# Moving the side pieces of an LSTM stage to other places, starting two chunks a round earlier, and building the length-1 weight sums in the layer that uses them

## The chip, the cores and the metric

One core of one Trainium2 chip runs the whole kernel as one program. The metric is the device time of that program in microseconds (us); lower is better. All matrices are float32.

The engines are named as the profile names them: PE (matmuls; PEld is its weight load), DVE (VectorE), ACT (ScalarE), POOL (GpSimd) and SP (SyncE, which only issues transfers here). Each takes its own instructions in the order of the program. A "manual schedule" in the kernel means that this order is the order in which the Python code emits the instructions.

## The reference, cut to what matters

Four residual layers act on x of shape 128 x 64 x 256 (8192 tokens of width 256). The change touches the second layer and its border with the first:

```python
# layer 1 (the second): h is relu(layernorm(x)), adj is 64 x 64
h = relu(einsum('ts,bsh->bth', adj, h @ Wg0 + bg0))
h = relu(einsum('ts,bsh->bth', adj, h @ Wg1 + bg1))
for p in range(1, 5):                       # four LSTMs, one after the other
    nw = T // p
    wins = h[:, :nw * p, :].reshape(B * nw, p, H)      # windows of p tokens
    last = lstm_last(Wih[p-1], Whh[p-1], bih[p-1], bhh[p-1], wins)
    h[:, arange(nw) * p + p - 1, :] = last             # overwrites the last token of a window
x = x + h
```

Layer 0 is a graph convolution with two batch norms, layer 2 causal attention, layer 3 masked attention with four heads. Each LSTM rewrites part of h before the next one reads it, so for one piece of data the four are a chain.

## The kernel before

The 8192 tokens are 16 chunks of 512. In layer 1 two chunks form a superchunk; there are eight, sc = 0 to 7. The LSTM code of a superchunk is the main stream. It is a Python generator that yields at 22 **places**, 0 to 21. At a place the main loop puts pieces of a second stream between the LSTM instructions: the two graph convolutions of the next superchunk's chunks, the residual sum of the last superchunk's, and the normalization that layer 2 will need. Length 1 has places 0 to 3, length 2 has 4 to 7, length 3 has 8 to 13, length 4 has 14 to 21.

```python
def convolutions(c):                      # 14 pieces, c0 to c13
    y, h = conv_tile(c)                   # c0: tag "cv", 2 buffers
    for m in range(KD): scaled(y, c, m)   #     two DVE operations
    mid = res.tile(...)                   #     two DVE transposes into mid
    far = put(mid, f"y{c}"); get(dst, far)      # store to DRAM, load back in token order
    nc.sync.dma_start(xs[c], xr[c])             # load x
    yield
    add_squares(xs[c], xs[c], dst); yield       # c1: DVE, needs both loads
    stats = ln_stats(xs[c], f"b{c}"); yield     # c2: DVE, then POOL (1/sqrt)
    yield from apply_halves(h, xs[c], stats, f"b{c}")   # c3, c4: ACT; c3 begins with nmr on DVE
    banks = aggregate(h, adjt_bd, f"b{c}"); yield       # c5: PE, 64 small matmuls
    ...copy on DVE...; yield                            # c6
    banks = product_v(c, y); yield                      # c7: PE, 3.4 us
    bounded(y, banks); yield                            # c8: DVE
    banks = product_u(c, y); yield                      # c9: PE, 3.4 us
    biased(h, banks); yield                             # c10: DVE
    banks = aggregate(h, adjt_bd, f"c{c}"); yield       # c11: PE
    for e, ps in enumerate(banks): to_hT(c, e, ps); yield   # c12, c13: ACT

def ahead(c):                             # 6 pieces, h0 to h5, for layer 2
    # h0 put, h1 load back, h2 statistics (DVE, POOL), h3 and h4 apply (ACT),
    # h5 four DVE transposes and a put

def residual(c, hT):                      # r0 transposes (DVE) and put, r1 load, r2 add
```

An LSTM step of length p works on "units", one for each gate and step. Each unit forms its product by a seven-product block scheme whose partial results lie in a few PSUM banks (tags x, y, z with two banks each), so that PE can go on only after ACT or DVE has read a bank:

```python
for s in range(1, p):
    last = s == p - 1
    B = [Unit(q, s) for q in (1, 3)]
    ...
    each(A, pe(5, "h"), do("copy", 5), pe(1), do("copy", 1), pe(3, "h"), pe(6, "x"), pe(6, "h"),
         pe(2, "h"), do("u4"), do("c11"), do("c12"))     # copy: ACT (L1155); u4, c11..: DVE (L1158)
    each(B, pe(5), do("copy", 5))
    each(A, do("act", 0), pe(7), do("c22"), do("act", 1))      # act: ACT (L1063)
    ...
    each(B, pe(1), do("copy", 1))
    yield                                                # a place in the middle of a step
    ...cells, tanh, new_state on DVE and ACT...
            new_state(s, 1, halves[1])
            ...
            new_state(s, 1, halves[0])
            if last: load_sets(2)
            else:    dh[2]()
    yield                                                # a place at the end of a step

def new_state(s, c, part):     # last step: the new h, written into the sequence
    ...
    nc.vector.tensor_mul(tokens(c, s, j), folded(gate(3, c, part)), folded(gate(2, c, part)))
```

The tables of places, and their use for superchunk sc:

```python
RESIDUAL = (0, 3, 4), (2, 5, 6)                 # chunks of sc - 1
CONV = (4, 4, 5, 6, 7, 8, 9, 10, 10), (6, 8, 9, 9, 10, 11, 12, 13, 14, 15, 16, 17, 18, 20)
                                                # first (A) and second (B) chunk of sc + 1
BEGUN = 13, 15, 16, 17, 18                      # first chunk of sc + 2
AHEAD = (4, 5, 10, 12, 14, 18), (6, 7)          # chunks of sc - 1
LATE = 4, 5, 6, 7                               # rest of the second chunk of sc - 2
```

The length-1 LSTM has no recurrent term. Its weights and their four block sums are `wih1`. They are made in layer 0, with those of the other lengths, and stored to DRAM; layer 1 loads them. At the border of the layers the product of two attention weights is also stored, and the first convolution reuses its memory:

```python
wanted = [(p, (wih_t, q), (whh_t, q)) for p in range(2, SKIP + 1) for q in GATES]
wanted[6:6] = [(1, (wih_t, GATES[0]), (wih_t, GATES[1]))]
wanted[7:7] = [(1, (wih_t, GATES[2]))]
...
nc.sync.dma_start(products_far, wqkv_sb[:, :, : 2 * D])     # in weight_products()
...
wih1 = w1.tile([P, 3, 7, P], F32, name="wih1")
for i, q in enumerate(GATES[:3]):
    nc.sync.dma_start(wih1[:, i], wfar[1, q])
```

Of the kernel before, what the change touches and what calls it, by code (L numbers as in the profile page):

```python
# [8 lines left out]
F32 = mybir.dt.float32  # L9
# [10 lines left out]
def kernel(  # L20
# [666 lines left out]
    with tc.manual_schedule(engines={mybir.EngineType.PE}):  # L687
# [30 lines left out]
        def weight_products():  # L718
            for m in range(KD):
                ps = bank(f"c1_{m}")  # L720
                nc.tensor.matmul(ps[:, :P], bg0_sb[:, m * P : (m + 1) * P], adjt_bd, start=True,
                                 stop=True)
                nc.scalar.copy(c1[:, m, :], ps[:, :P])
                nc.scalar.mul(nc1[:, m, :], ps[:, :P], -1.0)
            for a in range(KD):
                for dst, lhs, rhs in ((products[0], 0, wt[:, KD : 2 * KD, :]),
                                      (products[1], 2 * KD, wo_sb)):
                    ps = bank(f"wp_{a}_{lhs}")
                    for f in range(KD):
                        nc.tensor.matmul(ps[:, :D], wt[:, lhs + f, a * P : (a + 1) * P],  # L730
                                         rhs[:, f, :], start=(f == 0), stop=(f == KD - 1))
                    nc.scalar.copy(dst[:, a, :], ps[:, :D])
            nc.sync.dma_start(products_far, wqkv_sb[:, :, : 2 * D])
            ps = bank("c2")
            for k in range(KD):
                nc.tensor.matmul(ps[:, :D], c1[:, k, :], wg1_st[:, k, :], start=(k == 0),
                                 stop=(k == KD - 1))
            return ps

        def weight_sums(p, *sources):
            n = len(sources)
            name = "_".join(f"{p}{q}" for _, q in sources)
            w = stage.tile([P, 16, P], F32, tag="ws", name=f"ws_{name}", bufs=2)
            for i, (src, q) in enumerate(sources):
                nc.sync.dma_start(
                    w[:, 8 * i : 8 * i + 4, :].rearrange("p (k c) f -> p k (c f)", k=KD),
                    src[p - 1].rearrange("(k p) f -> p k f", p=P)[:, :, q * D : (q + 1) * D])
            yield  # L750
            v = w.rearrange("p (i b) f -> p i b f", i=2)[:, :n]
            for dst, a, b, op in ((4, 1, 3, OP.add), (5, 4, 0, OP.subtract), (6, 0, 1, OP.subtract),
                                  (7, 2, 5, OP.subtract)):
                nc.gpsimd.tensor_tensor(v[:, :, dst], v[:, :, a], v[:, :, b], op)
            if p == 1:
                for i, (_, q) in enumerate(sources):
                    far = dram.tile([P, 7, P], F32, tag=f"ws{p}{q}", name=f"wfar_{p}_{q}", bufs=1)
                    nc.sync.dma_start(far[:, :1], w[:, 8 * i : 8 * i + 1])
                    nc.sync.dma_start(far[:, 1:], w[:, 8 * i + 2 : 8 * i + 8])
                    wfar[p, q] = far  # L760
            else:
                far = dram.tile([P, 15, P], F32, tag=f"ws{p}{q}", name=f"wfar_{p}_{q}", bufs=1)
                nc.sync.dma_start(far[:, :9], w[:, :9])
                nc.sync.dma_start(far[:, 9:], w[:, 10:])
                wfar[p, q] = far
            yield

        wanted = [(p, (wih_t, q), (whh_t, q)) for p in range(2, SKIP + 1) for q in GATES]
        wanted[6:6] = [(1, (wih_t, GATES[0]), (wih_t, GATES[1]))]
        wanted[7:7] = [(1, (wih_t, GATES[2]))]  # L770
    tc.no_sync_barrier()


    with tc.manual_schedule(engines={mybir.EngineType.PE, mybir.EngineType.DVE,
# [2 lines left out]
        sevens[2].relu(2, 3, 0, 1)  # L777
        for c in range(2, NCH - 1):
            a, b, z = sevens[c], sevens.get(c + 1), sevens.get(c - 1)
            weights = [weight_sums(*wanted.pop(0)) for _ in range(1 + (len(wanted) == 7)) if wanted]  # L780
            for w in weights:
                next(w)
            a.product(2, "Z")
            if c == 2:
                a.begin()
# [36 lines left out]
            else:  # L822
                new_h1(c + 1)
                for k in range(KH):
                    relu2(c + 1, k)
            for w in weights:
                next(w)
            a.product(3, "Y")
            a.add(0, 1, "Y")
            if b:  # L830
# [38 lines left out]
    nc.sync.dma_start(bias2, bhh)  # L869

    wih1 = w1.tile([P, 3, 7, P], F32, name="wih1")
    for i, q in enumerate(GATES[:3]):
        nc.sync.dma_start(wih1[:, i], wfar[1, q])

    coming = [(p, q) for _ in range(NCH // SUP) for p in range(2, SKIP + 1) for q in GATES]
    wsets = {}
# [141 lines left out]

    BLOCKS = {1: (0, 8), 2: (2, 9), 3: (7, 14), 4: (3, 10), 5: (4, 11), 6: (5, 12), 7: (6, 13)}

    def lstm(p, hv, name):


        nb = hv.shape[3]
# [16 lines left out]
        def folded(t):  # L1041
            return t.rearrange("p (a b) -> p a b", b=inner)
# [16 lines left out]
        def gate(q, c, part=slice(0, n)):  # L1059
            return gates[:, q, c, part]  # L1060
# [5 lines left out]
        halves = [slice(0, m), slice(m, n)]  # L1066
        every = slice(0, n)

        def new_state(s, c, part):

            if s < p - 1:
                nc.vector.tensor_mul(hn[:, c, part], gate(3, c, part), gate(2, c, part))
            elif part == every:
                nc.vector.tensor_mul(natural(hv[:, c, cols(s), :]), columns_of(gate(3, c)),  # L1074
                                     columns_of(gate(2, c)))
            else:
                j = halves.index(part)
                nc.vector.tensor_mul(tokens(c, s, j), folded(gate(3, c, part)),
                                     folded(gate(2, c, part)))

        def operands_x(s):

# [111 lines left out]
        for s in range(1, p):  # L1194
# [48 lines left out]
            new_state(s, 1, halves[1])  # L1243
            if not last:
                dh[1]()
            new_state(s, 1, halves[0])
            if last:
                load_sets(2)
            else:
# [124 lines left out]
    def lstms(sc, hT):  # L1374
        hv = hT.rearrange("p k (t b) -> p k t b", t=T)

        def views(part):
            return {(k, j): part(hv[:, k, j * T // 2 : (j + 1) * T // 2, :]) for k in range(KD)
                    for j in range(2)}

        if sc:
            yield from single(views(lambda a: a.rearrange("p t b -> p (t b)")), CH, f"{sc}_1", range(4))
        else:
            for i in range(SUP):
                yield from single(views(lambda a: a[:, :, i * NB : (i + 1) * NB]), CH // 2, f"{sc}_1_{i}",
                                  (1, 3))
        for p in range(2, SKIP + 1):
            yield from lstm(p, hv, f"{sc}_{p}")

    def new_hT(sc):  # L1390

# [48 lines left out]


    RESIDUAL = (0, 3, 4), (2, 5, 6)
    CONV = (4, 4, 5, 6, 7, 8, 9, 10, 10), (6, 8, 9, 9, 10, 11, 12, 13, 14, 15, 16, 17, 18, 20)
    BEGUN = 13, 15, 16, 17, 18
    FIRST = (0, 2, 3, 4, 4, 5, 6, 7, 8, 9, 10, 11, 12, 12), (3, 6, 7, 8, 8, 13, 14, 15, 16, 17, 18, 19, 20, 20)
    AHEAD = (4, 5, 10, 12, 14, 18), (6, 7)
    LATE = 4, 5, 6, 7
    IDLE = {5: 4, 7: 18, 9: 10, 13: 14, 15: 8}
    FINAL = (4, 5, 10, 12, 12, 14), (6, 7, 11, 14, 14, 16)
    START = (0, 1, 0, 0, 0, 1, 0, 1, 1, 0, 0, 1, 1, 0, 1)  # L1450
# [2 lines left out]
    with tc.manual_schedule(engines={mybir.EngineType.PE, mybir.EngineType.DVE, mybir.EngineType.Pool,  # L1453
# [5 lines left out]
        for n, i in enumerate(START):  # L1459
# [5 lines left out]
                    keep_busy(fill, name)  # L1465
            next(convs[i])
            if n == 1:
                load_sets(6)
    banks_of("psum1", x=2, y=2, z=2, ps=2)
    tc.no_sync_barrier()  # L1470
    with tc.manual_schedule(engines={mybir.EngineType.PE, mybir.EngineType.DVE, mybir.EngineType.Pool,
                                     mybir.EngineType.Activation, mybir.EngineType.SP}):
        last = NCH // SUP - 1
        for sc in range(last + 1):
# [21 lines left out]
                for i in range(SUP):  # L1496
                    units((FINAL if sc == last else AHEAD)[i], aheads[(sc - 1) * SUP + i])
            if sc + 1 < last:
                units(BEGUN, convs[(sc + 2) * SUP])
            for n, _ in enumerate(lstms(sc, hTs[sc])):  # L1500
                for u in todo.pop(n, ()):
                    next(u)
# [537 lines left out]
```

## Time and profile before

| quantity | value |
|---|---|
| device time, median of 3 | 1962.3 us (1960.02 to 1969.14) |
| span of the profiled execution | 1964.6 us |
| PE busy | 1879.6 us, 96% of the span |
| DVE, ACT, POOL busy | 1263.7, 1015.8, 567.9 us |
| layer 1 LSTMs, sc = 0 to 7 | about 296 to 1590 us of the span |
| one middle superchunk | about 164 to 167 us |

A row of the timeline gives start, duration, engine, line, operation, what it writes and reads, and how many equal ones were merged. The bracket at its end is the time for which the engine stood idle before it, and the instruction that ended this idle time. "DMA" as the releaser means a transfer that landed. PEclk in the table of windows is the share of full TensorE clock that was granted.

### The profile page before, as it was taken

Reading aid. Unit: us, or ns where it says so; the run is one execution under the profiler, and the core shown is the slowest. Engines: PE = TensorE matmul, PEld = TensorE weight load, DVE = VectorE, ACT = ScalarE, POOL = GpSimd, SP = SyncE. Lnnn points to the kernel's source line nnn. Section 1 sums busy time; section 2 is a strip of 40 time slices with the busy share of each in tenths; the row PEclk is TensorE's granted clock in tenths of the full one; section 3 lists DMA queues with packets and bytes.
Section 4 is the critical chain, followed back from the end, with each engine's and each line's share of the span. In section 5 each row is a group of like instructions: output and inputs, shape, how many; then the busy total and the mean of one; then the engine's idle time right before and its main releaser. Section 6 shows DMA issues by size and latency. Waiting matters only on the chain.

```text
span 1964.6 us, 39217 instructions
## 1 busy us (share of the span) xinstructions
PE 1879.6 (96%) x15119; PEld 1494.1 (76%) x15119; DVE 1263.7 (64%) x3164; ACT 1015.8 (52%) x2309; POOL 567.9 (29%) x763
## 2 busy tenths in 40 slices
PE   8999979999999999999999999999999999999998
PEld 6877756886787788588678768858968976777776
DVE  6768635556556756666665666666565657667776
ACT  5766426456355445544645555554464544444453
POOL 5756512222212121222212212122132213223332
PEclk9999989999999999999999999999999999999999
DMA  3224552134432432443353233244235335444433
GB/s 111 75 65 177 196 212 71 75 113 141 139 113 103 118 125 81 145 145 113 124 177 113 92 115 134 85 145 145 81 124 166 100 93 164 143 141 130 151 115 113
DMA packets 112219, 244.23 MB, mean 124 GB/s; under 512 B 11552, under 2 KB 74912, under 8 KB 112032
## 3 DMA queue, kind: packets, MB, share of 16 engines
q1 hardware_dynamic: 111280, 240.37, 36.3%
q8 instruction: 120, 1.97, 0.4%
q0 software_dynamic: 320, 1.05, 0.2%
q14 instruction: 67, 0.55, 0.1%
q10 hardware_dynamic: 432, 0.30, 0.1%
HBM read 171.88 MB, written 69.80 MB: 123 GB/s over the span
## 4 chain that ended last, share of the span: by engine, by line
PE 69%; DVE 9%; ACT 5%; DMA 2%; issue 2%; POOL 1%; SPq 0%; DVEq 0%; ACTq 0%; POOLq 0%
PE x L1149 19%; PE z L1149 9%; PE g L1120 8%; PE v L1530 5%; PE y L1149 5%; PE x L1304 3%; PE p_q L1537 3%; PE u L924 3%; PE v L910 3%; PE X L1726 2%; PE y L1304 2%; DVE cell L1217 1%; DVE cell L1216 1%; PE Y L1726 1%; DVE gates L1158 1%
## 5 line engine op out<-in xcount | busy, mean ns | idle before, releaser
L1158 DVE TENSOR_TENSOR gates<-gates,x 128x128 f32<-128x128 f32 (+2 forms) x384 | 119.3, 322 | 323.7 <-PE x L1149 316.0
L1149 PE MATMUL x<-xd,wset 128*128 128x128 f32 (+2 forms) x1280 | 288.3, 313 | 37.4 <-ACT gates L1155 27.8
L1207 POOL TENSOR_TENSOR gates<-gates 128x512 f32<-128x512 f32 (+2 forms) x48 | 76.7, 1599 | 628.8 <-ACT gates L1063 628.8
L1149 PE MATMUL x<-hd,wset 128*128 128x128 f32 (+2 forms) x1152 | 248.5, 305 | 0.0
L1149 PEld LDWEIGHTS x<-xd,wset 128*128 128x128 f32 x1280 | 203.5, 191 | 58.3 <-ACT gates L1155 21.2
L1063 ACT ACTIVATE gates<-gates,bias 128x256 f32<-128x256 f32 (+4 forms) x384 | 169.9, 490 | 61.7 <-DVE gates L1158 59.3
L1149 PEld LDWEIGHTS x<-hd,wset 128*128 128x128 f32 x1152 | 186.7, 193 | 5.0
L1120 PE MATMUL g<-hT,wset 128*128 128x256 f32 (+2 forms) x576 | 184.1, 474 | 1.2 <-DVE hT L1074 1.1
L1120 PEld LDWEIGHTS g<-hT,wset 128*128 128x128 f32 x576 | 108.5, 190 | 70.0 <-issue 39.5
L1149 PE MATMUL z<-hs,wset 128*128 128x128 f32 (+2 forms) x768 | 155.6, 305 | 0.0
L1155 ACT COPY gates<-y 128x128 f32<-128x128 f32 (+2 forms) x192 | 53.4, 293 | 189.7 <-PE y L1149 189.0
L1149 PEld LDWEIGHTS z<-hs,wset 128*128 128x128 f32 x768 | 121.4, 193 | 3.3
L1107 ACT ACTIVATE gates<-g,bias 128x512 f32<-128x512 f32 (+2 forms) x144 | 76.9, 562 | 67.8 <-PE g L1120 67.3
L1158 DVE TENSOR_TENSOR gates<-gates,z 128x128 f32<-128x128 f32 (+2 forms) x384 | 104.8, 316 | 1.0 <-PE z L1149 0.9
L1155 ACT COPY gates<-x 128x128 f32<-128x128 f32 (+2 forms) x192 | 55.5, 297 | 87.6 <-PE x L1149 87.1
L1063 ACT ACTIVATE gates<-x,bias 128x128 f32<-128x128 f32 (+2 forms) x192 | 74.8, 390 | 50.2 <-PE x L1149 47.4
L1149 PE MATMUL z<-hT,wset 128*128 128x128 f32 (+1 forms) x512 | 97.1, 302 | 0.0
L1218 ACT ACTIVATE gates<-cell 128x256 f32<-128x256 f32 (+2 forms) x144 | 55.2, 384 | 70.2 <-DVE cell L1217 70.1
L1149 PE MATMUL x<-hs,wset 128*128 128x128 f32 (+2 forms) x384 | 84.9, 303 | 0.0
L313 POOL TENSOR_TENSOR xd<-hT 128x128 f32<-128x128 f32 (+3 forms) x57 | 38.4, 674 | 160.0 <-DVE hT L1074 100.5
L1149 PE MATMUL y<-hd,wset 128*128 128x128 f32 (+2 forms) x384 | 81.2, 314 | 0.0
L1149 PE MATMUL y<-xd,wset 128*128 128x128 f32 (+2 forms) x384 | 78.6, 307 | 2.1 <-ACT gates L1107 2.1
(324 smaller groups left out, 4291.0 us busy)
## 6 DMA issues: line engine op xcount, KB each, us to landing
wset<-wfar SPq DMA_DIRECT2D x96, 960.0 KB, 6.5
hT<-far_h SPq DMA_DIRECT2D x124, 128.0 KB, 3.2
far_h<-hm SPq DMA_DIRECT2D x16, 512.0 KB, 2.8
far_n<-xs SPq DMA_DIRECT2D x16, 512.0 KB, 4.2
xs<-far_n SPq DMA_DIRECT2D x64, 128.0 KB, 3.5
far_x<-xs SPq DMA_DIRECT2D x16, 512.0 KB, 3.0
x<-far_x SPq DMA_DIRECT2D x64, 128.0 KB, 3.2
xt<-in_x_dram SPq DMA_DIRECT2D x15, 512.0 KB, 4.0
```

What stands on the lines that cost most here:

```text
L910: nc.tensor.matmul(banks[m], wg0_sb[:, k, m * P : (m + 1) * P], agg[:, k, :], start=(k == 0), stop=(k == KD - 1))
L924: nc.tensor.matmul(banks[j // 2][:, j % 2, :], v[:, k, j * P : (j + 1) * P], wg1_sb[:, k, :], start=(k == 0), stop=(k == KD - 1))
L1063: nc.scalar.activation(gate(q, c, part), src, AF.Tanh if q == 2 else AF.Sigmoid, bias=bs[:, q * KD + c : q * KD + c + 1])
L1107: nc.scalar.activation(columns_of(gate(q, c)), natural(banks[q, c][:, :n].rearrange("p (w b) -> p w b", b=nb)), AF.Tanh if q == 2 else AF. ...
L1120: nc.tensor.matmul(banks[q, c][:, :n].rearrange("p (w b) -> p w b", b=nb), wsets[p, q][:, 2 * k + c, :], hv[:, k, : (nw - 1) * p + 1 : p, ...
L1149: nc.tensor.matmul(folded(self.psum(kind)), wsets[p, self.q][:, BLOCKS[kind][i], :], (ox[self.s] if part == "x" else oh)[kind], start=firs ...
L1155: nc.scalar.copy(gate(self.q, kind // 5, halves[kind // 5]), self.psum(kind))
L1158: nc.vector.tensor_add(gate(self.q, *dst), gate(self.q, *a), self.psum(kind))
L1207: nc.gpsimd.tensor_mul(gates[:, 0, :, :n], gates[:, 0, :, :n], gates[:, 2, :, :n])
L1304: nc.tensor.matmul(folded(ps(g, kind)), wih1[:, g, KINDS1[kind], :], right[kind], start=kind in (2, 5, 1), stop=True, skip_group_check=True)
L1530: nc.tensor.matmul(ps[:, i, :], hT[:, k, j, :], w[:, k, first : first + D], start=(k == 0), stop=(k == KD - 1))
L1726: nc.tensor.matmul(st[c, tag][:, i * CH // 2 : (i + 1) * CH // 2].rearrange("p (a n) -> p a n", n=P), w, st[c, "o7"][kind], start=first an ...
```

## The change

It has four parts.

1. The tables of places are rewritten. No place holds the statistics of a chunk together with the scaling that needs them, and several pieces move by one to six places.
2. Both chunks of sc + 2, not only the first, are begun one superchunk ahead: the first with pieces c0 to c3 (before: c0 to c4), the second with c0 and c1.
3. The very last state multiplication of length 4 runs on POOL instead of DVE where another superchunk follows.
4. The length-1 weight sums leave layer 0. Layer 1 loads the raw weights while its first convolutions run, and POOL forms the four sums there. The store of the attention products is issued from ACT's queue instead of SP's.

The place tables, and what lies at each place in a middle superchunk (A, B: chunks of sc + 1; A', B': of sc + 2; R: residual; H0, H1: the two chunks of sc - 1; L: the late chunk):

| place | before | after |
|---|---|---|
| 3 | R0.r1 | A.c4, B.c2, R0.r1 |
| 4 | L.h2, A.c5, A.c6, R0.r2, H0.h0 | A.c5, A.c6, B.c3, B.c4, R0.r2, H0.h0 |
| 5 | A.c7, R1.r1, L.h3, H0.h1 | L.h2, A.c7, R1.r1, H0.h1 |
| 6 | A.c8, B.c0, R1.r2, L.h4, H1.h0 | A.c8, R1.r2, L.h3, H1.h0 |
| 7 | A.c9, L.h5, H1.h1 | A.c9, H0.h2, H1.h1 |
| 8 | A.c10, B.c1 | A.c10, L.h4, H0.h3 |
| 9 | A.c11, B.c2, B.c3 | A.c11, L.h5 |
| 10 | A.c12, A.c13, B.c4, H0.h2 | A.c12, A.c13 |
| 11 | B.c5 | B.c5, A'.c0 |
| 12 | B.c6, H0.h3 | B.c6 |
| 13 | B.c7, A'.c0 | B.c7, A'.c1 |
| 14 | B.c8, H0.h4 | B.c8, H0.h4, A'.c2 |
| 15 | B.c9, A'.c1 | B.c9, H0.h5 |
| 16 | B.c10, A'.c2 | B.c10, A'.c3 |
| 17 | B.c11, A'.c3 | B.c11, B'.c0 |
| 18 | B.c12, H0.h5, A'.c4 | B.c12 |
| 19 | | B'.c1 |
| 20 | B.c13 | B.c13 |

The diff, cut to its core:

```diff
-            nc.sync.dma_start(products_far, wqkv_sb[:, :, : 2 * D])
+            nc.scalar.dma_start(products_far, wqkv_sb[:, :, : 2 * D])
...
-        wanted[6:6] = [(1, (wih_t, GATES[0]), (wih_t, GATES[1]))]
-        wanted[7:7] = [(1, (wih_t, GATES[2]))]
...
-    for i, q in enumerate(GATES[:3]):
-        nc.sync.dma_start(wih1[:, i], wfar[1, q])
+    def load_single():
+        rest = ...                        # the memory of an LSTM cell tile
+        for g, q in enumerate(GATES[:3]):
+            raw = wih_t[0].rearrange("(k p) (q f) -> p k q f", p=P, f=D)[:, :, q]
+            nc.sync.dma_start(wih1[:, g, 0], raw[:, 0, :P])
+            nc.sync.dma_start(rest[:, g], raw[:, 0, P:])
+            nc.sync.dma_start(wih1[:, g, 1:3], raw[:, 1].rearrange("p (c f) -> p c f", c=KD))
+        yield
+        w = wih1.rearrange("p g s f -> p s g f")
+        for dst, a, b, op in ((3, rest, w[:, 2], OP.add), (4, w[:, 3], w[:, 0], OP.subtract),
+                              (5, w[:, 0], rest, OP.subtract), (6, w[:, 1], w[:, 4], OP.subtract)):
+            nc.gpsimd.tensor_tensor(w[:, dst], a, b, op)
+        yield
...
-            new_state(s, 1, halves[0])
+            new_state(s, 1, halves[0], nc.gpsimd if follows and last else nc.vector)
...
-    CONV = (4, 4, 5, 6, 7, 8, 9, 10, 10), (6, 8, 9, 9, 10, 11, 12, 13, 14, 15, 16, 17, 18, 20)
-    BEGUN = 13, 15, 16, 17, 18
+    CONV = (3, 4, 4, 5, 6, 7, 8, 9, 10, 10), (3, 4, 4, 11, 12, 13, 14, 15, 16, 17, 18, 20)
+    BEGUN = (11, 13, 14, 16), (17, 19)
+    BEGUN_FIRST = (13, 15, 16, 18), (19, 21)              # used in sc = 0
-    AHEAD = (4, 5, 10, 12, 14, 18), (6, 7)
-    LATE = 4, 5, 6, 7
+    AHEAD = (4, 5, 7, 8, 14, 15), (6, 7)
+    LATE = 5, 6, 8, 9
...
+                singles = load_single()                   # n == 1 of the first convolutions
+                next(singles)
                 load_sets(6)
+            if n == 9:
+                next(singles)
```

## The prediction

> **What bounds the kernel now.** I read the busy times by engine first. PE is busy for 1879.6 of 1964.6 us, so the whole kernel has some 85 us of PE idle time, and the other engines matter only where they make PE wait. Then I cut the span by stage, with the table of windows (columns: stretch, its length, busy time and instructions of PE, PEld, DVE, ACT, POOL, then PEclk, DMA share, GB/s):
>
> ```profile
> 223.00:260.00 37.00, 26.73 (x114) 19.66 (x112) 17.74 (x40) 12.11 (x28) 13.66 (x19) 0.91 0.62 216
> 313.00:460.00 147.00, 142.62 (x1062) 120.59 (x1063) 82.93 (x240) 73.56 (x190) 33.68 (x47) 1.00 0.26 94
> 627.00:794.00 167.00, 159.66 (x1092) 129.21 (x1091) 106.56 (x282) 86.09 (x211) 38.23 (x51) 0.98 0.36 123
> 959.00:1123.00 164.00, 156.66 (x1092) 126.30 (x1091) 106.32 (x282) 86.11 (x211) 38.05 (x51) 1.00 0.36 125
> 1448.00:1590.00 142.00, 139.33 (x817) 115.44 (x815) 84.21 (x243) 80.77 (x196) 32.46 (x45) 1.00 0.35 111
> ```
>
> A middle superchunk loses about 7.3 us of PE (164 - 156.66), the first and last 3 to 4, the border of layers 0 and 1 about 10. DVE and ACT have room on average, so a wait can only come from their order. The timeline of PE alone gives each wait by name; one superchunk (sc = 3) has these, and they repeat to 0.02 us in sc = 1 to 5:
>
> ```profile
> 795.65 1.12 PE L1304 MATMUL x<-hT,wih 128*128 128x512 f32 x2 [0.90 <-ACT gates L1063]
> 868.11 1.49 PE L1149 MATMUL x<-xd,wset 128*128 128x168 f32 x4 [3.28 <-ACT gates L1155]
> 883.36 0.55 PE L1149 MATMUL x<-xd,wset 128*128 128x168 f32 x2 [0.85 <-DVE gates L1158]
> 931.64 0.68 PE L1149 MATMUL x<-xd,wset 128*128 128x128 f32 x4 [1.63 <-ACT gates L1155]
> 942.31 0.49 PE L1149 MATMUL x<-xd,wset 128*128 128x128 f32 x2 [0.43 <-DVE gates L1158]
> ```
>
> The full timeline around each says why. For the largest:
>
> ```profile
> 864.47 0.23 POOL L99 TENSOR_SCALAR rstd_b<-mv_b 128x4 f32<-128x4 f32 x1 [7.66 <-DVE mv_b L160]
> 864.78 1.04 POOL L100 TENSOR_TENSOR rstd_b<-rstd_b,mhalf 128x4 f32<-128x4 f32 x1
> 865.85 0.49 DVE L194 SCALAR_TENSOR_TENSOR nmr_b<-mv_b,rstd_b 128x4 f32<-128x4 f32 x1 [1.48 <-POOL rstd_b L100]
> 866.38 1.09 ACT L196 ACTIVATE cv<-xs,nmr_b,rstd_b 128x256 f32<-128x256 f32 x2 [5.66 <-DVE nmr_b L194]
> 867.38 0.47 ACT L1155 COPY gates<-y 128x168 f32<-128x168 f32 x2
> ```
>
> Place 9 holds c2 and c3 together. ACT, in order, stands 5.66 us at c3 for the chain DVE, POOL, DVE, and the copy that PE needs is behind it. At 931.64 (place 17) the same happens smaller: c3 waits for its nmr behind the end of the step on DVE, then takes 1.09 us ahead of the copies. At 883.36 and 942.31 (places 10 and 18) ACT has 1.94 or 1.06 us of c12/c13 and then 1.05 us of c4 before the sigmoids. At 795.65 the border of two superchunks: POOL's block differences for the next length 1 run beside the last DVE cells.
>
> The border of the layers hangs on one transfer:
>
> ```profile
> 251.47 0.60 SPq L733 DMA_DIRECT2D wqv_far<-wqkv_sb  x1
> 259.46 2.23 ACT L892 ACTIVATE cv<-z1a,sh_bn,sc_bn 128x512 f32<-128x512 f32 x3 [9.38 <-DMA wqv_far<-wqkv_sb]
> 260.33 3.57 PE L239 MATMUL at_b<-ident,cv 128*128 128x128 f32 x16 [10.12 <-ACT cv L892]
> ```
>
> **What the Trainium skill says.** (1) "TensorE: Matmul & The Clock Gate", section "HAM oscillation": idle gaps over about 3.4 us throttle the PE clock, and the part before it says that the watching window runs freely, so the effect of a gap depends on its phase. The trace agrees: after the same 3.28 us gap the 15 us around it have a granted clock of 0.77, 0.77 and 0.89 in sc = 1, 2, 3, and 1.00 in sc = 4 to 6. (2) "SBUF — State Buffer", "SBUF: two separate sides": POOL and a DVE operation with two SBUF inputs lock one shared port against each other. It agrees: a 128x256 cell operation takes 0.43 us alone (925.11) and 1.38 us beside POOL's differences (955.80). (3) "DMA: Bandwidth & Descriptors", "Issuing engines are not separate DMA queues": issuing from ACT saves only the sequencer's time. Here that time is the point: the store stands behind nine other issues of SP.
>
> **The change part by part.** PE's instructions are the same, so I count its gaps.
>
> Removed in a middle superchunk: place 9, 3.28. Place 10, 0.85: c4 leaves ACT, 1.05 us earlier, enough. Place 17, 1.63: c3 leaves; the y copies can follow PE. Place 18, 0.43: c4 leaves. Sum 6.2 us.
>
> New there:
> - Place 17 gets c0, on DVE 1.14 + 1.30 = 2.44 us (904.49, 905.66). DVE is free at 929.8 in the trace, so its first u4 is done at 929.8 + 2.44 + 0.29 = 932.5; without the old wait PE would want it at 932.1. About 0.5 us.
> - Place 8 gets H0.h3 whose statistics are at place 7. Statistics 2.1 us after 854.2, then POOL 1.3: nmr at 857.7, ACT done with h3 at 859.0, while the first sigmoids of length 3 began at 856.76. They now begin 2.2 us later; the z banks are read at 860.7 and 861.3 instead of when PE wants them (859.96 and 860.24). POOL's seven length-3 operands also start behind that 1/sqrt, and the last copy that PE reads ends at about 860.7. The two overlap: about 1.0 us.
> - Place 4 gets c3 and c4 of B, 2.1 us on ACT before the sigmoids of length 2. Their banks are wanted at 821.5 to 822.8 and would be read at 820.8 to 822.6: no wait, by a few tenths. The h products come at 827.6, after the 3.4 us c7, and absorb the rest.
> - Place 11 with c0 (DVE done at 889.7, next wanted at about 890.9), 14 with c2, and 19 with c1 look hidden. Place 15 loses 4.40 us of DVE waiting for the x load (916.19): c0 to c1 is now two length-3 places.
>
> Net 6.2 - 1.5 = 4.7 us; five superchunks (sc = 1 to 5) give 23.5. sc = 6 has no begun chunks: 4.1 - 1.0 = 3.1. sc = 0 keeps its 2.08 us wait (418.43, DVE at c1 for its load, still at places 13 and 15) and gets c0 at 19: -0.5.
>
> Border of superchunks, 7 times: 0.90 and 0.24 us of wait. POOL's state operation needs the last tanh, so the four differences now start behind it (about 959.6 instead of 953.3 in the trace's time). DVE then runs without the lock: 1.38, 0.93 and 1.35 us become 0.42, 0.42 and 0.28, so the last PSUM bank is read by about 958.6 and PE's L1304 runs on to 960.7. The first difference, 1.28 us, is ready at 960.9, the third at about 963.7, when PE wants it at 963.6. Wait 0.35 instead of 1.14: 0.8 each, 5.6.
>
> Clock: without a gap over 1.6 us I expect none of the three dips: (0.23 + 0.23 + 0.11) x 11.7 us of PE busy in each = 6.7.
>
> Border of layers: ACT can issue the store after its last copy at 250.1, and the three 448 KB loads no longer run beside it. A 512 KB transfer takes 2.8 to 4.2 us to land in the table of DMA issues (this one took 7.9), so it lands at about 254.3 and not 259.4. The early x load waits for it too and shifts alike: 5.2. The raw weights (768 KB) and four POOL sums of 128x384, about 1 us each scaled from 3.4 us for four of 128x256, fit before the first length 1 at 290: nothing on the path. Layer 0's own waits stay.
>
> Sum: 23.5 + 3.1 - 0.5 + 5.6 + 6.7 + 5.2 = 43.6, so 1918.7. I take off 1.6 for small waits that a hand count misses: **1920**.
>
> **The rivals.** (a) Waits move rather than go: places 4, 8 and 17 are denser now and my margins at 4 are tenths. If each costs 1.5 us more in six superchunks, 27 us are lost: about 1945. For it: the 0.5 and 1.0 that I found already. Against it: in the old trace the dense places that don't hold up ACT (5, 6, 7, 13) show no PE gap. (b) The POOL step delays all four differences: if it ends 2 us later than I think, seven borders cost 14 us: 1934. Against it: the lock is gone just then. (c) The clock dips elsewhere, or the border's transfer is replaced by the raw loads as the last release: 1927 and 1925. (d) All waits vanish: 5 x 1.5 + 1 + 2.5 more: about 1908.
>
> **Range and chances.** Most of the gain (23.5 + 3.1) is the removal of named, repeating waits, so "same time or slower" would need (a) and (b) at once. 80% range: 1907 to 1939. Two per cent faster means 1923.1, only 3 us above my number, which makes it little better than even: 0.58 faster, 0.40 within 2%, 0.02 slower.
>
> **What would show it.** In the new trace: no gap at c11 of length 3 (place 9) above 0.5 us; PEclk 1.00 in all superchunks; a period of about 159 us in the middle; a new gap of about 1 us at the first z product of length 3, with ACT's L1107 as its releaser; about 0.5 us at place 17, by DVE L1158; L1304's first y product on differences at most 0.4 us late, released by POOL; ACT's first scaling near 254 us. I am wrong if ACT or POOL holds PE at places 4 or 8 for more than 2 us, if the border gap grows beyond 1.1 us, or if the store still lands at 258 or later.

## The result, and the profile after

The changed kernel takes **1907.77 us** (1907.27 to 1908.97) where the kernel before takes 1962.31 us: a ratio of 0.9717, 95% interval 0.9693 to 0.9742. Predicted were 1920 us with a range that began at 1907, so the time lies at its very edge: 54.5 us were gained and 42.3 predicted. What bounds the kernel was read rightly. One step of the sum failed ("Layer 0's own waits stay"), and several of its terms had the wrong size.

The two profiled spans differ by 59.2 us. Of these, 49.3 are idle time of PE (85.0 us before, 35.7 now) and 9.9 are its busy time (1879.6 us before), although PE's 15119 matmuls are the same and come in the same order:

```profile
span 1905.4 us, 39237 instructions
PE 1869.7 (98%) x15119; PEld 1489.5 (78%) x15119; DVE 1238.2 (65%) x3157; ACT 1017.2 (53%) x2309; POOL 578.4 (30%) x766
```

In the table of windows, the two windows of middle superchunks whose rows stand in the prediction now read as follows (same columns):

```profile
627.00:794.00 167.00, 166.28 (x1122) 131.96 (x1121) 109.94 (x295) 93.04 (x223) 42.60 (x54) 1.00 0.38 131
959.00:1123.00 164.00, 163.30 (x1125) 132.56 (x1124) 105.42 (x287) 89.23 (x218) 41.95 (x52) 1.00 0.37 129
```

PE loses 0.7 us in such a stretch, before it was 7.3, and PEclk is 1.00 in both. The period from one superchunk to the next is 156.88 us (672.68 to 829.56, the same matmul of two superchunks). In the timeline of PE, one superchunk keeps only two waits above 0.1 us, both at place 8 where length 3 begins. They repeat within 0.01 us in sc = 1 to 6:

```profile
825.82 0.89 PE L1152 MATMUL y<-xd,wset 128*128 128x168 f32 x4 [0.29 <-ACT gates L1110]
829.56 0.84 PE L1152 MATMUL y<-hd,wset 128*128 128x168 f32 x4 [0.32 <-DVE hd L313]
```

All five waits that the prediction listed are gone. At the border of the layers the store is issued and lands earlier:

```profile
244.16 0.61 ACTq L733 DMA_DIRECT2D wqv_far<-wqkv_sb  x1
247.38 2.22 ACT L895 ACTIVATE cv<-z1a,sh_bn,sc_bn 128x512 f32<-128x512 f32 x3 [3.25 <-DMA wqv_far<-wqkv_sb]
248.25 3.68 PE L239 MATMUL at_b<-ident,cv 128*128 128x128 f32 x16 [3.67 <-ACT cv L895]
```

The first transposes stand at 248.25 instead of 260.33: 12.1 us. That is more than the 5.2 us predicted for this border. Most of the surplus is not in these three lines but ahead of them, in layer 0.

The stages of the two profiles, laid beside the terms of the prediction (the profiled run of before is 4.2 us above its median, that of after 0.5 us below; a superchunk ends here where the next one's first product on a difference, y<-xd,wih, starts):

| stage | gained | predicted, with the border of superchunks and the clock |
|---|---|---|
| up to the first length 1 | 12.7 | 5.2 |
| sc = 0 | 1.5 | -0.5 + 0.8 |
| sc = 1, 2, 3, 4, 5 | 10.0, 9.8, 8.4, 7.0, 7.1 | 8.2, 8.2, 6.8, 5.5, 5.5 |
| sc = 6 | 4.9 | 3.1 + 0.8 |
| sc = 7, layers 2 and 3 | -0.6, -1.5 | 0 |

Two errors are to be seen here: 7.5 us before the first length 1, and 1.5 to 1.8 us in each middle superchunk. The last row is a loss of 2.1 us that no step foresaw. The 0.6 belongs to part 3: sc = 7 has a new wait of 0.70 us (g<-hT at 1403.74, released by DVE), and a wait of 0.70 to 0.73 us stands there in all nine profiles of this document with POOL's product and in none of the eight without it. The 1.5 is no more than scatter: what follows the LSTMs of sc = 7 takes between 372.1 and 375.1 us in the seventeen profiles, whatever the kernel.

### The profile page after: what moved, and what is told of

Read it like the earlier page. It is cut to its first block, busy times and chain, and to the rows that moved or that the text cites. A ratio compares the mean times of both kernels' runs of the same rounds, so it can differ in the third digit from the quotient of the medians.

```text
span 1905.4 us, 39237 instructions
## 1 busy us (share of the span) xinstructions
PE 1869.7 (98%) x15119; PEld 1489.5 (78%) x15119; DVE 1238.2 (65%) x3157; ACT 1017.2 (53%) x2309; POOL 578.4 (30%) x766
## 4 chain that ended last, share of the span: by engine, by line
PE 82%; DVE 8%; ACT 4%; POOL 2%; issue 2%; DMA 1%; SPq 0%; DVEq 0%; ACTq 0%
PE x L1152 22%; PE z L1152 11%; PE g L1123 7%; PE y L1152 5%; PE v L1539 5%; PE x L1307 3%; PE p_q L1546 3%; PE y L1307 3%; PE X L1735 3%; PE v L913 3%; PE X L423 2%; PE X L499 2%; PE u L927 2%; PE Y L1735 1%; PE Y L423 1%
## 5 line engine op out<-in xcount | busy, mean ns | idle before, releaser
L1110 ACT ACTIVATE gates<-g,bias 128x512 f32<-128x512 f32 (+2 forms) x144 | 72.3, 557 | 17.7 <-PE g L1123 17.6
L1554 POOL TENSOR_TENSOR s<-s,mx 128x256 f32<-128x256 f32 (+2 forms) x33 | 40.4, 1225 | 129.6 <-DVE mx L1553 121.8
```

The lines of the kernel that those rows point to most:

```text
L1110: nc.scalar.activation(columns_of(gate(q, c)), natural(banks[q, c][:, :n].rearrange("p (w b) -> p w b", b=nb)), AF.Tanh if q == 2 else AF. ...
```

## The experiments

**The parts alone.** Each of the first three takes one part of the change into the kernel before. The store and the length-1 sums (part 4):

```diff
-            nc.sync.dma_start(products_far, wqkv_sb[:, :, : 2 * D])
+            nc.scalar.dma_start(products_far, wqkv_sb[:, :, : 2 * D])
-        wanted[6:6] = [(1, (wih_t, GATES[0]), (wih_t, GATES[1]))]
-        wanted[7:7] = [(1, (wih_t, GATES[2]))]
+        ... load_single() in layer 1, as in the change
```

> The kernel before with part 4 alone (weight sums of length 1 moved to layer 1, store of the attention products on ACT's queue). Theory 1: the extra weight sets made POOL's queue slip in layer 0, and PE waited there; with the border transfer this part is worth about 12.5 us: 1950, and PE has no wait over 0.3 us between 205 and 236 us. Theory 2 (the sum on record): layer 0's waits stay and only the border gains, about 5 to 6.5 us: 1956 to 1957.

1953.07 us, ratio 0.9946 (0.9927 to 0.9965): 10.6 us gained, twice the predicted 5.2. No wait of PE above 0.3 us is left between 205 and 236 us, as theory 1 said.

The places and the chunks begun ahead (parts 1 and 2):

```diff
-    CONV = (4, 4, 5, 6, 7, 8, 9, 10, 10), (6, 8, 9, 9, 10, 11, 12, ...)
-    BEGUN = 13, 15, 16, 17, 18
+    CONV = (3, 4, 4, 5, 6, 7, 8, 9, 10, 10), (3, 4, 4, 11, 12, ...)
+    BEGUN = (11, 13, 14, 16), (17, 19)
     ... AHEAD, LATE as in the change
```

> The kernel before with the new tables of places and the second chunk begun ahead (parts 1 and 2). Theory 1: the waits of 3.28, 0.85, 1.63 and 0.43 us in each middle superchunk become one of about 0.6 us at the start of length 3, and the clock dips go: 5 x 5.6 + 3.5 + about 6 = 37 us, 1925. Theory 2: part of the gain belongs to the other two parts (DVE freed by POOL at the border of superchunks), and the gain is 27 us or less: 1935 or more.

1931.36 us, ratio 0.9825 (0.9811 to 0.984): 34.3 us. PE keeps the two small waits of place 8, the waits of layer 0 and those of the border of superchunks, 0.89 and, 1.36 us later, 0.24 us:

```profile
936.80 1.13 PE L1304 MATMUL x<-hT,wih 128*128 128x512 f32 x2 [0.89 <-ACT gates L1063]
```

The last state product on POOL (part 3):

```diff
-            new_state(s, 1, halves[0])
+            new_state(s, 1, halves[0], nc.gpsimd if follows and last else nc.vector)
```

> The kernel before with the last state product of length 4 on POOL and nothing else (part 3). Theory 1: POOL's differences start later, DVE's cells aren't locked out beside them, and both waits at a border of superchunks (0.90 and 0.24 us) go without a new one: 7 x 1.1 = 8 us, 1954. Theory 2: the differences are now late for the fifth product and a wait of at least the same size takes their place: 1962 or more.

1959.06 us, ratio 0.996 (0.9944 to 0.9976): 7.8 us, and both border waits are gone. In this profile the clock dips behind the 3.28 us gap in five of six superchunks instead of three, so part of the gain may be hidden. The reverse, the changed kernel without this part:

> The changed kernel with the last state multiplication of length 4 back on DVE. Theory 1 (the parts add): the two waits of 0.90 and 0.24 us at each border of two superchunks come back, seven times: about 8 us more than the changed kernel, 1915.5. Theory 2 (with the new places DVE has less behind the last cells and the border waits are gone anyway): under 3 us more, 1908 to 1911.

1918.84 us, ratio 0.9754 (0.9718 to 0.979). The waits of 0.90 and 0.24 us are back at each border. Theory 1's mechanism holds. The loss against the changed kernel is larger than its 8 us: 11.1 in the medians, 11.4 in the spans (10 against the later run of the changed kernel below; these were not run side by side). The two profiles say the same: between the borders lie 158.48 us instead of 156.82, so a border costs 1.66 us, of which 1.14 are recorded as waits. Each ratio taken on 1962.31 us, the three parts sum to 34.3 + 10.6 + 7.8 = 52.7 us beside 54.5 measured: they add, within their intervals.

**Which half of part 4, and why.** Only the store on ACT's queue:

> The kernel before with only the store of the attention products issued from ACT's queue; the length-1 sums stay in layer 0 with their three loads. Theory 1 (two separate gains at the border of the layers: the transfer, and the waits of layer 0 that the length-1 sums cause): the store is issued near 250.1 instead of 251.5 us, no weight loads stand between it and its landing, it lands near 254, the first transposes of the convolution begin near 255; the three waits of layer 0 between 211 and 235 us (0.5, 2.7 to 3.2, 0.4) stay. Gain about 5 us, time about 1957. Theory 2 (the waits of layer 0 come from transfers in SP's queue as well): these waits go too, gain about 10, time about 1952.

Ratio 1.0005 (0.9987 to 1.0023), 1968.82 us: no gain, and both theories fail. The timeline at the border:

```profile
250.93 0.61 ACTq L733 DMA_DIRECT2D wqv_far<-wqkv_sb  x1
258.97 2.22 ACT L892 ACTIVATE cv<-z1a,sh_bn,sc_bn 128x512 f32<-128x512 f32 x3 [8.29 <-DMA wqv_far<-wqkv_sb]
```

The store is issued 0.54 us earlier than before and still takes 8 us to land, with the three loads of 448 KB beside it. The expectation took these loads away in thought, though the kernel still issues them. So ACT's queue was not the point. The other half, only the sums moved and the store left on SP:

> The kernel before with only the length-1 sums moved to layer 1; the store stays on SP's queue. Theory 1: without the nine length-1 transfers SP has issued everything by about 234 us, so it issues the store as soon as ACT's last copy allows, and without the three loads beside it the store lands in about 3 us: the same as when ACT issues it. Layer 0's waits go too. Gain about 10.5 us, time about 1952. Theory 2 (ACT's queue is what makes the store early): the first transposes begin about 4 us later than in the changed kernel, gain about 6, time about 1956.

1958.67 us, ratio 0.9951 (0.9934 to 0.9969), 9.6 us: within the intervals the whole of part 4. SP issues the store at 244.53, against 244.16 from ACT's queue in the changed kernel, and it lands in 3.1 us (table of DMA issues) in both.

What the sums did to layer 0 is seen in the kernel before, in its full timeline:

```profile
209.90 0.34 SPq L763 DMA_DIRECT2D wfar<-ws  x1
210.82 0.85 SPq L747 DMA_DIRECT2D ws<-in_wih_t_dram  x1
215.90 3.34 POOL L754 TENSOR_TENSOR ws<-ws 128x256 f32<-128x256 f32 x4 [4.80 <-DMA ws<-in_wih_t_dram]
219.20 1.26 POOL L314 TENSOR_TENSOR t<-z1b,z1a 128x512 f32<-128x512 f32 x1
220.49 0.37 ACT L506 COPY z1a<-Y 128x256 f32<-128x256 f32 x1 [4.37 <-POOL t L314]
220.92 1.13 PE L499 MATMUL Y<-z1b,w_sums 128*128 128x256 f32 x4 [2.66 <-ACT z1a L506]
```

POOL stands 4.80 us for the load of a weight set. The block difference that layer 0's matmuls need is behind these sums in its queue, ACT's copy behind that, and PE last. The loads of this set were issued from 210.82 us on. They stand in SP's queue behind the store of the set before (209.90), which had to wait for POOL's sums of that set, done at 209.87. All this comes after the one iteration that forms two weight sets. With two stage buffers (`bufs=2`) a load can also have to wait until an earlier set has been stored: between 195 and 250 us SP stands for this five times, 8.7 us in all. The test keeps every sum, load and store, and puts the double iteration last, with the store on ACT's queue as in the run with the store alone:

```diff
-        wanted[6:6] = [(1, (wih_t, GATES[0]), (wih_t, GATES[1]))]
-        wanted[7:7] = [(1, (wih_t, GATES[2]))]
+        wanted += [(1, (wih_t, GATES[0]), (wih_t, GATES[1])), (1, (wih_t, GATES[2]))]
-            weights = [... for _ in range(1 + (len(wanted) == 7)) if wanted]
+            weights = [... for _ in range(1 + (len(wanted) == 2)) if wanted]
```

> The kernel before with the store on ACT's queue, and with the two length-1 sets of layer 0 put at the end of the list, so that the two sets of one iteration are formed in the last iteration instead of the seventh before the end; POOL's work, loads and stores are the same in number. Theory 1 (layer 0's waits come from the one iteration with two sets, whose loads wait for the stores of a tag with two buffers and then hold POOL's queue): the waits of about 2.7 and 0.4 us go or shrink to under 1.5 in sum, and the time lies 2 to 4 us under the kernel with only the store moved: about 1954. Theory 2 (it is the amount of sums and transfers in layer 0, wherever they stand): the waits stay at 3 to 4 us, only elsewhere before 236 us: about 1957.

1961.88 us, ratio 0.9979 (0.9965 to 0.9993), beside 1968.82 of the store alone. No wait of PE above 0.2 us is left between 205 and 236 us: theory 1 holds. Five profiles side by side (us from the start of the span):

| kernel | first weight transpose (layer 0 done) | store issued | landed | first transposes of layer 1 |
|---|---|---|---|---|
| before | 235.37 | 251.47 | 259.46 | 260.33 |
| store on ACT | 235.63 | 250.93 | 258.97 | 259.84 |
| store on ACT, double iteration last | 230.11 | 247.28 | 253.67 | 254.53 |
| sums moved, store on SP | 230.13 | 244.53 | 247.74 | 248.61 |
| changed | 229.75 | 244.16 | 247.38 | 248.25 |

The first column shows the slip: 5.5 us by the order of the same work alone. Beside the third row, the last two show what moving the sums adds. The store lands in 3.2 us instead of 6.4, and its issue is 2.8 to 3.1 us earlier. The reason for the latter is POOL's queue again: in the run of the third row the last sums run there until 243.19 us, a 1/sqrt of layer 0 follows, DVE stands 5.76 us for it, and behind DVE's statistics ACT comes to the copies that the store needs at 246.04 us. With the sums moved and the store on SP it comes to them at 241.56. A third stage buffer would test the chain from another side. It was not tried, and it would not take a load out of its place behind a store in SP's queue.

**Place 9, the largest wait.** First, in the kernel before, c1 and c2 of B one place earlier, so that c2 no longer shares place 9 with c3:

```diff
-    CONV = ..., (6, 8, 9, 9, 10, 11, ...)
+    CONV = ..., (6, 7, 8, 9, 10, 11, ...)
```

> The kernel before, with only c1 and c2 of the second chunk one place earlier (7 and 8 instead of 8 and 9), so that the statistics are no longer in one place with the scaling (c3, still at 9). Theory 1: the wait for the chain DVE, POOL, DVE goes, but c3's 1.09 us still stand ahead of the copies, as at place 17: the wait at place 9 falls from 3.28 to about 1.5 us, and the clock dips of sc = 1 to 3 go with it: 6 x 1.8 + 6.5 = 17 us, 1945. Theory 2: the clock dips don't depend on this one wait: 11 us, 1951.

1965.78 us, ratio 1.0002 (0.999 to 1.0014): nothing gained, against both theories. The timeline says why: the statistics now hold DVE's first cells of length 3, which stand behind them. The wait at place 9 did shrink, to between nothing and 1.70 us, but one of 0.79 to 3.05 us came at place 8.

```profile
857.30 0.18 DVE L160 BATCH_NORM_AGGREGATE mv_b<-st_b 128x2 f32<-128x6 f32 x1
857.40 0.89 DVE L1113 TENSOR_TENSOR cell<-gates 128x336 f32<-128x336 f32 x2
857.90 0.48 ACT L1114 ACTIVATE gates<-cell 128x336 f32<-128x336 f32 x1 [3.61 <-DVE cell L1113]
860.00 1.29 PE L1149 MATMUL y<-hd,wset 128*128 128x168 f32 x4 [2.35 <-DVE hd L313]
```

So the question was asked again from the changed kernel, by putting pieces back to place 9. First the scalings alone, then the statistics too:

```diff
-    CONV = ..., (3, 4, 4, 11, 12, ...)
+    CONV = ..., (3, 9, 10, 11, 12, ...)      # c3 at 9, c4 at 10
+    CONV = ..., (9, 9, 10, 11, 12, ...)      # second kernel: c2 and c3 at 9, c4 at 10
```

> The changed kernel with the two scalings c3 and c4 of B put back to places 9 and 10; its statistics c2 stay at place 3, so that nmr is ready five places earlier. Theory 1 (the 3.28 us at place 9 came from the chain of the statistics, with ACT standing in line for it): ACT was idle for 5.66 us there, so a scaling of 1.09 us whose nmr is ready costs PE at most 0.4 us at place 9; at place 10 the 0.85 us of before come back, because c4 stands with c12 and c13 ahead of the sigmoids. About 1.0 to 1.3 us in each of six superchunks: 1914 to 1916. Theory 2 (any scaling at place 9 costs its own duration or more): 1.1 plus 0.85 in each of six, 12 us: 1919 to 1920.

> The changed kernel with the statistics c2 and the scaling c3 of B both at place 9 and c4 at place 10, as in the kernel before; all else as changed. Theory 1: the wait of 3.28 us at place 9 and the 0.85 us at place 10 come back in six superchunks, 25 us, and some of the dips of the clock with them: 1933 to 1940; the difference to the kernel with only c3 and c4 moved back is 18 us or more. Theory 2: c2 adds under 1 us to each superchunk, so the difference is under 6 us.

With c3 and c4 back: 1921.38 us, ratio 0.9769 (0.9749 to 0.9788). PE waits 0.88 us at place 9 and 0.85 at place 10, close to what theory 2 said. ACT was free (its 2.13 us of idle time end at c3), but c3 begins with nmr on DVE (a small operation that makes the offset of the normalization), and DVE comes to it only behind the four hd differences of the step:

```profile
835.89 0.33 DVE L316 TENSOR_TENSOR hd<-hs,hd 128x168 f32<-128x168 f32 x1
836.14 0.15 DVE L194 SCALAR_TENSOR_TENSOR nmr_b<-mv_b,rstd_b 128x4 f32<-128x4 f32 x1
836.33 1.09 ACT L196 ACTIVATE cv<-xs,nmr_b,rstd_b 128x256 f32<-128x256 f32 x2 [2.13 <-DVE nmr_b L194]
838.06 0.84 PE L1152 MATMUL x<-xd,wset 128*128 128x168 f32 x4 [0.88 <-ACT gates L1158]
```

With c2 there as well: 1949.66 us, ratio 0.9917 (0.9891 to 0.9944), 28.3 us more. Theory 1 holds in kind, but the time is above its 1933 to 1940, and the wait is 4.49 us, not 3.28:

```profile
844.92 0.42 DVE L159 BATCH_NORM_STATS2 st_b<-xs 128x6 f32<-128x256 f32 x1
848.61 0.49 DVE L194 SCALAR_TENSOR_TENSOR nmr_b<-mv_b,rstd_b 128x4 f32<-128x4 f32 x1 [1.47 <-POOL rstd_b L100]
849.14 1.09 ACT L196 ACTIVATE cv<-xs,nmr_b,rstd_b 128x256 f32<-128x256 f32 x2 [5.65 <-DVE nmr_b L194]
850.86 1.49 PE L1152 MATMUL x<-xd,wset 128*128 128x168 f32 x4 [4.49 <-ACT gates L1158]
```

From the first statistics to the first copy are 5.2 us, as in the kernel before (862.16 to 867.38). The chain has its length wherever PE stands; here PE reaches the bank 1.2 us sooner after DVE's differences. So of 4.49 us, 3.61 are statistics and 1/sqrt, and 0.88 the scaling. Six times 3.61 are 21.7 us. The rest of the 28.3 is slow matmuls: x4 take 1.49, 1.33 and 1.12 us behind this wait and 0.73 otherwise. In the superchunk shown, the matmul that follows them starts 1.5 us later than in the run with the scalings alone; against it stand 0.4 us of a place 8 wait that is gone. The granted clock of the 15 us around it is 0.89 in all six superchunks.

**Place 8, the wait that is left.** In the changed kernel, h3 at place 12 instead of 8:

```diff
-    AHEAD = (4, 5, 7, 8, 14, 15), (6, 7)
+    AHEAD = (4, 5, 7, 12, 14, 15), (6, 7)
```

> The changed kernel with H0.h3, the scaling for layer 2, at place 12 instead of 8. Theory 1 (its statistics at place 7 and the scaling behind them make the last two waits of 0.30 and 0.32 us at the start of length 3): both go in sc = 1 to 6, gain about 3.7 us: 1904. Theory 2 (they come from A.c10, L.h4 or the operands of length 3 on DVE): they stay, 1907 to 1908.

1912.83 us, ratio 0.9726 (0.9705 to 0.9747): 4 to 5 us slower instead of 3.7 faster. The two waits are gone, as theory 1 said, and a longer one has taken their place, in all six superchunks:

```profile
824.05 2.23 ACT L1110 ACTIVATE gates<-g,bias 128x336 f32<-128x336 f32 x4 [2.19 <-PE g L1123]
825.75 1.28 DVE L1116 TENSOR_TENSOR cell<-gates 128x336 f32<-128x336 f32 x2 [1.11 <-ACT gates L1110]
827.38 1.52 POOL L1095 COPY xd<-hT 128x168 f32<-128x168 f32 x3
828.95 1.41 PE L1152 MATMUL z<-xd,wset 128*128 128x168 f32 x8 [1.55 <-POOL xd L1095]
```

Freed from h3, ACT gives DVE its first cells earlier, and these now run beside POOL's seven operands of length 3. A difference on POOL takes 0.54 us alone and up to 0.81 here, the three copies 1.52 us instead of 0.86. This fits the lock that "SBUF — State Buffer", section "SBUF: two separate sides", describes: an operation of POOL and one of DVE with two inputs from SBUF shut each other out. In the changed kernel h3 had kept DVE away from POOL just long enough. That leaves the 1/sqrt of h2, which stands ahead of the operands on POOL. With h2 at place 10 as well:

```diff
-    AHEAD = (4, 5, 7, 8, 14, 15), (6, 7)
+    AHEAD = (4, 5, 10, 12, 14, 15), (6, 7)
```

> The changed kernel with H0.h2 at place 10 and H0.h3 at place 12, as before the change; the other four parts of H0 as changed. With h3 alone at 12 the waits of 0.30 and 0.32 us at place 8 turned into one of 1.55 us at the first z product of length 3, for the last of POOL's seven operands. Theory 1 (POOL is late because the statistics at place 7 put 1.3 us of 1/sqrt ahead of the operands, and because ACT's sigmoids, no longer held by h3, let DVE's first cells run beside the operands): with the statistics at place 10 the operands start 1.3 us earlier and PE waits for nothing at the start of length 3, 3.7 us less than the changed kernel: 1904, and 9 us less than with h3 alone. Theory 2 (only the two sharers of the port matter, the 1/sqrt doesn't): the wait stays above 1 us, 1910 to 1913.

**1902.40 us**, ratio 0.9677 (0.9662 to 0.9691). PE has no wait above 0.2 us from 452 to 1398 us:

```profile
821.92 0.86 POOL L1095 COPY xd<-hT 128x168 f32<-128x168 f32 x3
822.74 2.23 ACT L1110 ACTIVATE gates<-g,bias 128x336 f32<-128x336 f32 x4 [1.97 <-PE g L1123]
825.93 1.30 PE L1152 MATMUL z<-xd,wset 128*128 128x168 f32 x8
```

The first set of operands is finished as ACT's first sigmoid begins. The changed kernel itself, run beside it:

> The changed kernel as it is, beside the two above on the same chip, as their measure: 1907 to 1910. Ratio to the kernel before about 0.972.

1908.79 us, ratio 0.9709 (0.9693 to 0.9725). So the step is worth 6.4 us and not 3.7. From the first product of length 3 to the first on hd takes 9.67 us now (818.58 to 828.25) and took 10.97 (818.59 to 829.56). Place 8 therefore cost 1.31 us per superchunk, of which only 0.62 are recorded as waits. The rest is matmuls that take longer while they wait: y<-xd x4 0.89 instead of 0.73, z<-xd x8 1.46 instead of 1.30.

**A better version.** First h3 at 12 together with two steps in sc = 0, A'.c0 at 12 instead of 13 and the second chunk's c3 and c4 at 10 instead of 8:

> The kernel with h3 at place 12, and in sc = 0 also A'.c0 at place 12 instead of 13 and the second chunk's c3 and c4 at place 10 instead of 8, to take away the two waits of 1.71 us (DVE at c1 for its x load) and 1.30 us (ACT's scalings ahead of the sigmoids of length 3) that sc = 0 still has. If both are caused as said: 3 us less than with h3 alone, about 1901. If DVE or ACT meets the same pieces elsewhere: 1903 to 1905.

1910.64 us, ratio 0.9716 (0.9696 to 0.9736): the wait for the x load (1.71 us) went, the other turned into the same 1.56 us of POOL. Then with all statistics away from the operands, in sc = 0 too:

```diff
-    BEGUN_FIRST = (13, 15, 16, 18), (19, 21)
-    FIRST = ..., (3, 6, 7, 8, 8, 13, 14, ...)
-    AHEAD = (4, 5, 7, 8, 14, 15), (6, 7)
+    BEGUN_FIRST = (12, 15, 16, 18), (19, 21)
+    FIRST = ..., (3, 6, 9, 10, 10, 13, 14, ...)
+    AHEAD = (4, 5, 10, 12, 14, 15), (6, 7)
```

> The kernel with h2 and h3 at places 10 and 12, and in sc = 0 also A'.c0 at place 12 and the second chunk's c2, c3, c4 at places 9, 10, 10, so that no statistics stand ahead of the operands of length 3 there either. Theory 1: the waits of 1.71 and 1.30 us in sc = 0 go as well: 3 us less than h2 and h3 alone, 1901. Theory 2 (place 9 or 10 of sc = 0 is then too dense on DVE or ACT): 1903 to 1906.

**1897.38 us**, ratio to the kernel before 0.965 (0.9636 to 0.9665), 11.4 us less than the changed kernel beside it. Both waits of sc = 0 are gone. It beats both kernels.

## Why the prediction was right or wrong

**Right: what bounds the kernel, and what removes it.** The five named waits were most of what a middle superchunk lost, and all five went. The wait at place 9 is the chain DVE, POOL, DVE with ACT in line for it, as read: 3.61 us for it in the pair of experiments.

**Wrong: "Layer 0's own waits stay."** This is the step that failed. It put 0 us where 5.6 were gained, most of the 7.5 us missing before the first length 1. The waits (2.66 us at 220.92 among them) were taken as layer 0's own, without following them back to POOL L754, whose sums the change removes in part. The change ends the double iteration, and layer 0 is done 5.6 us earlier. The order alone gives 5.5 in the run with the double iteration last.

**Half right: the store.** From layer 0's end to the first transposes takes 18.5 us instead of 24.96, a gain of 6.5 beside 5.2; 4.8 of it lie in the landing (3.2 instead of 8.0 us), 1.7 in the issue. But the reason given with the skill, in the section "Issuing engines are not separate DMA queues" of "DMA: Bandwidth & Descriptors", was the wrong half. "Here that time is the point" is refuted by the store alone on ACT's queue (0.54 us earlier, no gain in time). The page's own sentence, that issuing elsewhere saves only the sequencer's time, was the better guide. The sums moved, with their three loads gone from beside the store, were the point: SP then issues it as early as ACT.

**Mis-sized: the new waits of a superchunk.** Since PE's matmuls come in the same order in both kernels, the start of each can be laid beside the start of the same one in the other kernel. A step in the difference is what a place gains or loses. Place 17 was put at 0.5 us and costs 0.32, in the way that was predicted. DVE is busy with c0 from 891.01, reads the x bank behind it, and PE's next x product starts when the first reading ends. Only 0.06 us of this are recorded as idle:

```profile
893.27 0.45 DVE L1161 TENSOR_TENSOR gates<-gates,x 128x128 f32<-128x128 f32 x2
893.57 0.49 PE L1152 MATMUL x<-xd,wset 128*128 128x128 f32 x2
```

The border's residue was put at 0.35. There is none at six of the seven borders, and 0.26 us at the first (449.26, released by POOL). The differences of the next length 1 follow POOL's state product at once, and the first is there before PE wants it:

```profile
917.85 0.45 POOL L1081 TENSOR_TENSOR hT<-gates 128x128 f32<-128x128 f32 x1 [6.20 <-ACT gates L1221]
918.26 1.27 POOL L313 TENSOR_TENSOR xd<-hT 128x512 f32<-128x512 f32 x1
919.88 2.74 PE L1307 MATMUL y<-xd,wih 128*128 128x512 f32 x6
```

Place 8 was put at 1.0 and cost 1.3. Its causes were named rightly (the sigmoids behind h3, the operands behind the 1/sqrt), and the runs added that taking away the first alone makes it worse (the second alone was not tried). Together 1.85 us were predicted and 1.6 found.

**Left out: what a wait costs beyond itself.** The prediction counted only idle time. By the starts of the matmuls, the old waits of sc = 4, where the clock did not dip, were worth more: 3.54 us for the 3.28 of place 9, 0.98 for 0.86 (place 10), 1.89 for 1.61 (place 17), 0.54 for 0.43 (place 18) and 1.64 for the 0.90 and 0.24 of the border. That is 8.6 for 7.3. Part of it is seen in the rows: the first matmuls behind a wait are recorded longer (0.84 instead of 0.73, 0.55 instead of 0.45, 1.13 instead of 0.91). With the 1.6 of the new waits, 7.0 us are gained in sc = 4, where 5.5 were predicted: 1.3 of the difference are the old waits, 0.2 the new ones.

**Right in kind, not in size: the clock.** No wait over 0.33 us is left in sc = 1 to 6 and PEclk is 1.00 there. But 6.7 us was the size in one profile only. The 3.28 us gaps were followed by x4 matmuls of 1.49 us in three of six superchunks before, in three of six with only the sums moved, in five of six with only the POOL product moved, and in none (0.84 to 0.92) with part 4 alone. In 40 executions the kernel before spreads from 1957.4 to 1973.1 us, and its time goes with the granted clock (0.997 in one of 1957.85 us, 0.987 in one of 1972.66). The changed one spreads over 2 us.

**The rivals.** (a) waits that move: seen at places 8 and 17, in sum smaller than counted. (b) came at the first border alone, with 0.26 us. (c) the clock did not dip in the middle superchunks (1.00 from 452 to 1399 us). (d), all waits gone at 1908, was nearest in time, but for another reason: small waits stayed while layer 0 gave more.

## What to carry to other kernels

Follow every wait back through all in-order queues before calling it a stage's own. A load that stands behind a store in one queue can surface as a wait two engines later, and a change elsewhere can remove it. Where two kernels have the same matmuls in the same order, compare their starts: the recorded idle time understated the waits of a superchunk here. A piece of work that needs a chain over several engines must not stand ahead of another's work in any of these queues. Moving it one place only hands the wait to the next queue, while several places away it was free here.

## What the runs showed of the hardware that was not expected

- The same gap of 3.28 us halves the speed of the next matmuls in some superchunks and not in others (1.49 or 0.84 us for x4, against 0.73 with no wait); a gap of 4.49 us did so in all six, with a granted clock of 0.89 over 15 us. "TensorE: Matmul & The Clock Gate", section "HAM oscillation", puts the limit at about 3.4 us. The second agrees with it; the first, which lies just below, shows a chance and not a threshold.
- A 512 KB store lands in 3.1 us without the loads and in 7.9 us beside 1.3 MB of them, from either queue.
- An ACT piece can shield POOL: taking 1.09 us of ACT work away at place 8 made PE wait 1.55 instead of 0.62 us, because DVE then ran beside POOL.
